# Banded attention before a routed feed-forward: q and k as two float32r pieces on two row tiles of TensorE

## The chip, the cores and the metric

One core of a Trainium2 chip runs the kernel. A core has five engines that work side by side and wait for each other by semaphores: TensorE (PE in the profile, with its weight loads as PEld), VectorE (DVE), ScalarE (ACT), GpSimd (POOL) and SyncE (SP), which here issues most DMA transfers. Matrix products land in a memory of their own, PSUM; everything else lives in SBUF, the memory that the engines share, or in DRAM. The metric is the time of one execution on the device, in microseconds (us).

## What is computed

The input is 16 sequences of 512 tokens and 128 features. Attention with 16 heads of 8 features, in which a token sees only tokens at most 128 away, is followed by a second stage that picks experts by keys. Only the first stage is touched by the change. Cut to what matters:

```python
x = L0_attn_x                                    # 16 x 512 x 128, f32
qkv = einsum('btc,oc->bto', layernorm(x), w_qkv) # q, k, v: 16 heads of 8
attn = einsum('bhqd,bhkd->bhqk', q, k) / sqrt(8)
attn = where(abs(key - query) > 128, -1e9, attn)
out = einsum('bhqk,bhkd->bhqd', softmax(attn), v)
x = x + einsum('btc,oc->bto', out, w_proj)
x = x + ffn(layernorm(x), ...)                   # batch norm, top-8 keys, experts: the second stage
```

## The kernel before

The attention stage works in units `n`: one sequence `b` and one group `g` of four heads, so 16 x 4 = 64 units, and in steps `u` of 128 tokens, four to a unit. Since the band is 128 wide, a block of 128 queries meets two or three blocks of 128 keys: 256 columns at the two ends of a sequence, 384 in the middle.

The scores are wanted in the precision of f32, but the products run in bf16. So `prepare` (L339) projects q and k of a whole sequence in f32 on TensorE, ScalarE copies them out (L348), and GpSimd splits each into three bf16 pieces whose sum is the f32 value (L362 to L370: copy, subtract, copy, subtract, each over 128 x 512). `write` (L353) stores the pieces in DRAM, and `lay` (L388) fetches them, for a unit, into the tiles `qst` and `kst`, so that the partitions hold every pairing of a q piece with a k piece: 3 x 3 x 8 = 72 rows, all four heads side by side along the free axis, three fetches for q and three for k. Rows 96 to 98 of `qst` are set to zero by one more transfer (L403), and the rows of `kst` beside them hold ones. There are six buffers of each tile; each is cleared once in whole by GpSimd (`clear`, L269).

Softmax runs in two passes over the scores. In the first, `greatest` (L409) multiplies a block of queries with its keys (a tile `s_ps` of PSUM, three buffers), and VectorE adds the band's mask and takes the row maximum in one operation (L424), which writes a scratch tile `masked` and, through a second short instruction that reads the accumulator, one column of `mx`. GpSimd negates the maxima and splits them in three bf16 pieces (`greatest_pieces`, L430), TensorE transposes these (four transposes, L447), ScalarE copies the result out (L449), and three small transfers put it in rows 96 to 98 of `qst` (L451). In the second pass, two units later, `exponentials` (L453) multiplies the keys with the queries (`e_ps`, three buffers), and the extra rows, met by the ones of `kst`, subtract the maximum; ScalarE takes the exponential (L466) into `pT`, and GpSimd clears what is outside the band (L474). `weigh` (L479) multiplies with v in f32, four heads on four column tiles of 32, into `o_ps`; `divide` (L497) transposes the result and divides by the sum.

One loop (L548 to L584) writes the order of all this out by hand. A step issues, on TensorE's queue, one s product of unit n + 2, two e products of unit n, one s product, the four weighings of an earlier step, then s, e, e, s again; after that come the pieces of maxima at u = 0, their rows at u = 1, the division at u = 2, and one piece of other work (projections and norms of sequences ahead, the output projection, the second norm). `lay` for unit n + 4 stands at u = 2. Work on TensorE and GpSimd keeps this order (`keep_in_program_order`), and a queue stands still behind its first waiting instruction. SP issues the writes, the fetches and the rows of maxima in one queue.

Of the kernel before, what the change touches and what calls it, by code (L numbers as in the profile page):

```python
# [10 lines left out]
F32 = mybir.dt.float32  # L11
BF16 = mybir.dt.bfloat16
I32 = mybir.dt.int32
# [7 lines left out]
P = 128  # L21
# [22 lines left out]
def kernel(  # L44
# [108 lines left out]
    with ExitStack() as at:  # L153
# [27 lines left out]
        for c, w in enumerate((wqT, wkT, wvT, wprojT)):  # L181
            wt = wt_ps[:, c * P : (c + 1) * P]
            if c < 2:

                w, wt = w.rearrange("p (d h) -> p d h", d=DK), wt.rearrange("p (h d) -> p d h", d=DK)
            nc.vector.tensor_copy(w, wt)
# [72 lines left out]
        NR = 96  # L259
        zeros = fix.tile([P, T], BF16, name="zeros")  # L260
        nc.gpsimd.memset(zeros, 0.0)
# [4 lines left out]
        qst = [fix.tile([P, 4, T], BF16, name=f"qst_{i}") for i in range(NBUF)]  # L266
        kst = [fix.tile([P, 4, T], BF16, name=f"kst_{i}") for i in range(NBUF)]

        def clear(i):  # L269

            nc.gpsimd.memset(qst[i].bitcast(F32), 0.0)
            nc.gpsimd.memset(kst[i].bitcast(I32), 0x3F803F80)
# [66 lines left out]
        def prepare(b):  # L339
# [13 lines left out]
            def write(what):  # L353

                via = dr.tile([3, P, T], BF16, tag=f"{what}v", name=f"{what}v_{b}")
                nc.sync.dma_start(via.rearrange("s c t -> c s t"), pieced[what, b])
                pieced[what, b] = via

            for what, full in fulls:
                pc = w2.tile([P, 3, T], BF16, tag="pc", name=f"{what}p_{b}")  # L360
                rest = w2.tile([P, T], F32, tag="rest", name=f"rest_{what}_{b}")
                pool("tensor_copy", pc[:, 0], full)  # L362
                yield
                pool("tensor_tensor", rest, full, pc[:, 0], ALU.subtract)
                yield
                pool("tensor_copy", pc[:, 1], rest)
# [3 lines left out]
                pool("tensor_tensor", pc[:, 2], rest, pc[:, 1], ALU.subtract)  # L370
# [17 lines left out]
        def lay(n):  # L388
# [4 lines left out]
            for what, st in (("q", qst[n % NBUF]), ("k", kst[n % NBUF])):  # L393
                src = pieced[what, b].rearrange("s (d h) t -> s d h t", d=DK)
                for i in range(3):
                    side = src[i if what == "q" else slice(0, 3)]
                    if what == "q":
                        side = bc(side, 0, 3)
                    nc.sync.dma_start(
                        st[3 * i * DK : 3 * i * DK + 3 * DK], side[:, :, 4 * g : 4 * g + 4]  # L400
                    )

            nc.sync.dma_start(qst[n % NBUF][NR : NR + 3], bc(zeros[0:3], 1, 4))  # L403
# [5 lines left out]
        def greatest(n, t):  # L409

            q, k = qst[n % NBUF], kst[n % NBUF]
            if t == 0:
                tops[n] = w2.tile([P, NQ, 4], F32, tag="mx", name=f"mx_{n}")
# [3 lines left out]
            for h in range(4):  # L417
                s_ps = ps_s.tile([P, 3, P], F32, tag="s", name=f"s_ps_{n}_{t}_{h}")
                s = s_ps.rearrange("p u k -> p (u k)")[:, 0:w]
                mm(  # L420
                    s, lhsT=q[:, h, t * P : (t + 1) * P], rhs=k[:, h, k0 : k0 + w],
                    start=True, stop=True,
                )
                nc.vector.tensor_tensor_reduce(  # L424
                    masked[:, 0:w], s, band.rearrange("p u k -> p (u k)")[:, from_u : from_u + w],
                    1.0, LOWEST, ALU.add, ALU.max, tops[n][:, t, h : h + 1],
                )
                yield

        def greatest_pieces(n):  # L430

            top = tops.pop(n)
            mp = w2.tile([P, NQ, 3, 4], BF16, tag="mp", name=f"mp_{n}")
            rest = w2.tile([P, NQ, 4], F32, tag="mr", name=f"mr_{n}")
            pool("tensor_scalar_mul", rest, top, -1.0)
            pool("tensor_copy", mp[:, :, 0], rest)
            pool("tensor_tensor", rest, rest, mp[:, :, 0], ALU.subtract)
            pool("tensor_copy", mp[:, :, 1], rest)
            pool("tensor_tensor", mp[:, :, 2], rest, mp[:, :, 1], ALU.subtract)
            tops[n] = mp  # L440

        def greatest_rows(n):

            mp = tops.pop(n)
            mT_ps = ps_m.tile([12, NQ, P], BF16, tag="m", name=f"mT_ps_{n}")
            for t in range(NQ):
                tr(mT_ps[:, t], mp[:, t].rearrange("p s h -> p (s h)"), ident_bf)  # L447
            mT = w2.tile([12, T], BF16, tag="mT", name=f"mT_{n}")
            nc.scalar.copy(mT, mT_ps.rearrange("r t q -> r (t q)"))  # L449
            for i in range(3):  # L450
                nc.sync.dma_start(qst[n % NBUF][NR + i : NR + i + 1], mT[4 * i : 4 * i + 4])  # L451

        def exponentials(n, u):  # L453


            q, k = qst[n % NBUF], kst[n % NBUF]
            ts = near(u)
            q0, w = ts[0] * P, len(ts) * P
            pT = w3.tile([P, 4, 3 * P], F32, tag="pT", name=f"pT_{n}_{u}")
            for h in range(4):  # L460
                e_ps = ps_e.tile([P, T], F32, tag="e", name=f"e_ps_{n}_{u}_{h}")
                mm(
# [609 lines left out]
```

## Time and profile before

| | |
|---|---|
| median of 3 runs | 1540.49 us (1539.85 to 1541.01) |
| span of the profiled execution | 1534.9 us |
| busy: PE / DVE / ACT / POOL | 1418.6 / 1347.5 / 1212.3 / 1094.3 us |
| first score product on PE | at 38.08 us |
| last masked maximum on DVE | ends at 714.3 us |
| masked maximum L424, all 1024 | 497.4 us busy, 486 ns each in the mean |
| exponential L466, all 1024 | 390.6 us busy, 436 ns each |
| s products, 1024 / e products, 1024 | 312.9 / 225.0 us busy, 307 / 301 ns each |
| rows fetched into qst, kst | 192 transfers each, 96 KB each |

The span is that of one execution that the profiler took, from its first to its last instruction; the runs are timed from outside. Busy time is the union of an engine's instructions. The records of matrix products overlap, since products are pipelined: a product's record lasts longer than the time until the next one may start, so throughput is read from start to start, not from the mean duration. An f32 product shows as two records, a bf16 one as one. A group of the profile gives line, engine, operation, tiles (out<-in), shapes and count, then busy time and mean, then the idle time of the engine before it and who ended it.

### The profile page before, as it was taken

What the parts mean: (1) busy time and instruction counts of PE and PEld (TensorE: products, weight loads), DVE (VectorE), ACT (ScalarE), POOL (GpSimd) and SP (SyncE); (2) the same over time, 40 slices, a digit from 0 to 9 for tenths busy, and PEclk for the clock granted to TensorE, in tenths of its full rate; (3) what the DMA queues carried; (4) which work ended last, traced back from release to release, by engine and by line L of the source; (5) the groups of instructions that cost most, each with busy time, mean ns of one, the idle gap of its engine ahead of it and who ended that gap; (6) DMA issues with size and microseconds to landing.
All of it is one profiled execution on the core that took longest, in us unless ns stands there. A gap on an engine that the chain in (4) does not pass through costs nothing.

```text
span 1534.9 us, 49438 instructions
## 1 busy us (share of the span) xinstructions
PE 1418.6 (92%) x16880; PEld 839.3 (55%) x16880; DVE 1347.5 (88%) x7999; ACT 1212.3 (79%) x2596; POOL 1094.3 (71%) x1706
## 2 busy tenths in 40 slices
PE   3899999999999999988689999999999999999998
PEld 1344454444444444443356666666666666666666
DVE  6778888878888888886599999999999999999994
ACT  1477777777777777778499999999999999999973
POOL 8366766667766667655287788878787888878875
PEclk9999999999999999999799999999999999999999
DMA  6243332222232222321000000000000000000000
GB/s 179 73 106 100 92 92 79 79 74 78 82 96 87 86 84 73 99 65 51 28 8 4 13 13 16 16 10 16 10 17 16 10 16 9 17 16 10 9 3 23
DMA packets 53580, 75.00 MB, mean 49 GB/s; under 512 B 5840, under 2 KB 39888, under 8 KB 53200
## 3 DMA queue, kind: packets, MB, share of 16 engines
q1 hardware_dynamic: 52496, 71.59, 16.1%
q8 instruction: 133, 2.18, 0.6%
q14 instruction: 119, 0.97, 0.2%
q10 hardware_dynamic: 832, 0.26, 0.1%
HBM read 49.28 MB, written 20.97 MB: 46 GB/s over the span
## 4 chain that ended last, share of the span: by engine, by line
DVE 48%; PE 2%; issue 1%; ACT 1%; POOL 0%; ACTq 0%
DVE idx L624 11%; DVE row L624 9%; DVE place L624 6%; DVE top L624 6%; DVE mine L624 5%; DVE best L624 4%; DVE x_ps L624 3%; DVE num L624 2%; DVE upper L624 1%; DVE zs L624 1%; PE up_ps L624 1%; PE dn_ps L624 0%; PE w_ps L624 0%; ACT L624 0%; POOL word L624 0%
## 5 line engine op out<-in xcount | busy, mean ns | idle before, releaser
L424 DVE CUSTOM_DVE_ANT_0 masked<-s_ps,band 128x384 bf16<-128x384 f32 (+1 forms) x1024 | 497.4, 486 | 126.0 <-PE s_ps L168 18.7
L466 ACT ACTIVATE pT<-e_ps 128x384 f32<-128x384 f32 (+1 forms) x1024 | 390.6, 436 | 152.8 <-PE e_ps L168 148.7
L172 POOL TENSOR_SCALAR_AFFINE_SELECT pT<-pT 128x512 f32<-128x512 f32 x384 | 238.3, 637 | 219.7 <-ACT pT L466 219.2
L168 PE MATMUL s_ps<-kst,qst 128*128 128x384 bf16 (+1 forms) x1024 | 312.9, 307 | 37.6 <-DVE mx L424 21.6
L624 POOL TENSOR_TENSOR cols<-mine,wT 64x512 f32<-64x512 bf16 x256 | 269.7, 1053 | 26.3 <-ACT row L624 6.9
L624 PE MATMUL w_ps<-cols,row 128*64 128x32 f32 x8192 | 257.3, 223 | 12.8 <-POOL cols L624 12.6
L624 PEld LDWEIGHTS w_ps<-cols,row 128*64 128x64 f32 x8192 | 249.4, 138 | 31.5 <-POOL cols L624 26.7
L624 POOL TENSOR_TENSOR g<-g,gel 128x512 f32<-128x512 f32 x128 | 163.6, 1278 | 102.2 <-ACT g L624 102.2
L168 PE MATMUL e_ps<-qst,kst 128*128 128x384 bf16 (+1 forms) x1024 | 225.0, 301 | 6.2 <-ACT pT L466 4.2
L168 PEld LDWEIGHTS <-qst 128*128 128x128 bf16 x1024 | 100.4, 98 | 197.1 <-issue 169.2
L168 PE MATMUL o_ps<-pT,vaug 128*32 128x384 f32 (+1 forms) x2048 | 191.6, 446 | 0.4 <-POOL pT L172 0.4
L624 DVE FIND_INDEX8 idx<-top,sim 128x8 uint32<-128x32 f32 x1024 | 166.2, 185 | 0.0
L624 ACT ACTIVATE row<-off_p,one 128x512 f32<-128x512 bf16 x256 | 165.9, 749 | 0.0
L624 ACT ACT_TABLE_LOAD x122 | 156.5, 1283 | 2.1
L624 DVE TENSOR_TENSOR row<-x_ps,nums_p 128x1024 f32<-128x1024 f32 x128 | 150.1, 1214 | 0.0
L624 ACT ACTIVATE off_p<-off_ps 128x512 bf16<-128x512 f32 x256 | 132.7, 602 | 18.1 <-PE off_ps L624 18.0
L624 PE MATMUL up_ps<-g,key_out_sb 64*128 64x256 f32 (+2 forms) x1152 | 146.2, 380 | 0.0
L624 PE MATMUL dn_ps<-xt,key_inT 128*64 128x256 f32 x1024 | 126.0, 389 | 2.2 <-ACT sim L624 1.3
L168 PEld LDWEIGHTS <-kst 128*128 128x128 bf16 x1024 | 98.9, 98 | 46.7 <-issue 21.1
L624 PE MATMUL off_ps<-p_bf,ident_bf 128*128 128x512 bf16 x256 | 97.5, 381 | 19.7 <-ACT p_bf L624 19.6
L624 PEld LDWEIGHTS dn_ps<-xt,key_inT 128*64 128x64 f32 x1024 | 68.5, 138 | 79.1 <-ACT row L624 43.2
L624 DVE MAX8 top<-sim 128x8 f32<-128x32 f32 x1024 | 106.6, 176 | 2.9 <-ACT sim L624 2.9
(145 smaller groups left out, 2365.0 us busy)
## 6 DMA issues: line engine op xcount, KB each, us to landing
qst<-qv SPq DMA_DIRECT2D x192, 96.0 KB
kst<-kv SPq DMA_DIRECT2D x192, 96.0 KB
qv<-qp SPq DMA_DIRECT2D x16, 384.0 KB
kv<-kp SPq DMA_DIRECT2D x16, 384.0 KB
x<-in_L_attn_x_dram SPq DMA_DIRECT2D x16, 256.0 KB
xT<-xiT SPq DMA_DIRECT2D x16, 256.0 KB
xt<-xT SPq DMA_DIRECT2D x16, 256.0 KB
out_dram<-o_sb SPq DMA_DIRECT2D x16, 256.0 KB
```

The source lines that it names most:

```text
L168: tc.keep_in_program_order(nc.tensor.matmul(*args, **kw))
L172: tc.keep_in_program_order(getattr(nc.gpsimd, op)(*args, **kw))
L424: nc.vector.tensor_tensor_reduce(masked[:, 0:w], s, band.rearrange("p u k -> p (u k)")[:, from_u : from_u + w], 1.0, LOWEST, ALU.add, ALU. ...
L466: nc.scalar.activation(pT[:, h, 0:w], e_ps[:, 0:w], AF.Exp)
L624: return lambda *args, **kw: tc.keep_in_program_order(op(*args, **kw))
```

## The change

q and k are split in two pieces of float32r (4 bytes) in place of three of bf16: copy and subtract on GpSimd, two operations in place of four. The pairings take 2 x 2 x 8 = 32 rows. Two heads lie above each other: one in rows 0 to 31, one from row 64 on, and two such pairs side by side along the free axis, so that a product of one head uses one of two row tiles of 64 of TensorE's array. One row of zeros against minus ones (row 32 or 96) makes a product 33 rows; two more rows, for the pieces of the maxima, make it 35 in the second pass. The order of products in a step is s, e, e, s as before, and takes the row tiles 0, 1, 0, 1 in turn. k is written to DRAM twice, so that one fetch per row tile brings both copies. The maxima are no longer negated, go in two pieces, and are transposed by one product of 128 columns with an identity in float32r; two transfers in place of three place them. The transfer of zeros is gone; `clear` sets one or three rows at a time, four memsets in place of two for a buffer. The weights of q and k are reordered so that heads come out in the new order.

```diff
 BF16 = mybir.dt.bfloat16
+F32R = mybir.dt.float32r
 I32 = mybir.dt.int32
...
             if c < 2:
-                w, wt = w.rearrange("p (d h) -> p d h", d=DK), wt.rearrange("p (h d) -> p d h", d=DK)
+                w = w.rearrange("p (g j d r) -> p g j d r", g=NG, j=2, r=2)
+                wt = wt.rearrange("p (g r j d) -> p g j d r", g=NG, j=2, r=2)
             nc.vector.tensor_copy(w, wt)
...
-        NR = 96
-        zeros = fix.tile([P, T], BF16, name="zeros")
-        nc.gpsimd.memset(zeros, 0.0)
+        NR, NPC = 32, 2
+        ident_r = fix.tile([P, P], F32R, name="ident_r")
+        nc.vector.tensor_copy(ident_r, ident)
         masked = fix.tile([P, 3 * P], BF16, name="masked")
         NU, NBUF = B * NG, 6
-        qst = [fix.tile([P, 4, T], BF16, name=f"qst_{i}") for i in range(NBUF)]
-        kst = [fix.tile([P, 4, T], BF16, name=f"kst_{i}") for i in range(NBUF)]
+        qst = [fix.tile([P, 2, T], F32R, name=f"qst_{i}") for i in range(NBUF)]
+        kst = [fix.tile([P, 2, T], F32R, name=f"kst_{i}") for i in range(NBUF)]
+        mps = [fix.tile([P, P], F32R, name=f"mp_{i}") for i in range(2)]
+        for mp in mps:
+            nc.gpsimd.memset(mp.bitcast(F32), 0.0)
         def clear(i):
-            nc.gpsimd.memset(qst[i].bitcast(F32), 0.0)
-            nc.gpsimd.memset(kst[i].bitcast(I32), 0x3F803F80)
+            for j in (NR, NR + P // 2):
+                nc.gpsimd.memset(qst[i][j : j + 1].bitcast(F32), 0.0)
+                nc.gpsimd.memset(kst[i][j : j + 1 + NPC].bitcast(F32), -1.0)
         clear(0)
...
             def write(what):
-                via = dr.tile([3, P, T], BF16, tag=f"{what}v", name=f"{what}v_{b}")
-                nc.sync.dma_start(via.rearrange("s c t -> c s t"), pieced[what, b])
+                times = 1 if what == "q" else 2
+                via = dr.tile([NG * 2, NPC, times, 2 * DK, T], F32, tag=f"{what}v", name=f"{what}v_{b}")
+                pc = pieced[what, b].bitcast(F32)
+                for i in range(NPC):
+                    for c in range(times):
+                        nc.sync.dma_start(via[:, i, c], pc[:, i])
                 pieced[what, b] = via
             for what, full in fulls:
-                pc = w2.tile([P, 3, T], BF16, tag="pc", name=f"{what}p_{b}")
-                rest = w2.tile([P, T], F32, tag="rest", name=f"rest_{what}_{b}")
+                pc = w2.tile([P, NPC, T], F32R, tag="pc", name=f"{what}p_{b}")
+                yield
                 pool("tensor_copy", pc[:, 0], full)
                 yield
-                pool("tensor_tensor", rest, full, pc[:, 0], ALU.subtract)
-                yield
-                pool("tensor_copy", pc[:, 1], rest)
                 if what == "k":
...
                 yield
-                pool("tensor_tensor", pc[:, 2], rest, pc[:, 1], ALU.subtract)
+                pool("tensor_tensor", pc[:, 1], full, pc[:, 0], ALU.subtract)
                 pieced[what, b] = pc
...
             for what, st in (("q", qst[n % NBUF]), ("k", kst[n % NBUF])):
-                src = pieced[what, b].rearrange("s (d h) t -> s d h t", d=DK)
-                for i in range(3):
-                    side = src[i if what == "q" else slice(0, 3)]
+                for j in range(2):
+                    side = pieced[what, b][2 * g + j].rearrange("i c (d r) t -> (i c d) (r t)", r=2)
                     if what == "q":
-                        side = bc(side, 0, 3)
-                    nc.sync.dma_start(
-                        st[3 * i * DK : 3 * i * DK + 3 * DK], side[:, :, 4 * g : 4 * g + 4]
-                    )
-            nc.sync.dma_start(qst[n % NBUF][NR : NR + 3], bc(zeros[0:3], 1, 4))
+                        side = bc(side, 0, 2)
+                    nc.sync.dma_start(st[P // 2 * j : P // 2 * j + NR].bitcast(F32), side)
         def near(t):
             return [u for u in (t - 1, t, t + 1) if 0 <= u < NQ]
-        def greatest(n, t):
-            q, k = qst[n % NBUF], kst[n % NBUF]
-            if t == 0:
-                tops[n] = w2.tile([P, NQ, 4], F32, tag="mx", name=f"mx_{n}")
+        def tile_of(j, rows):
+            return slice(P // 2 * j, P // 2 * j + rows)
+        def greatest(n, t, r, j):
+            q, k, rows = qst[n % NBUF], kst[n % NBUF], tile_of(j, NR + 1)
+            if t == r == j == 0:
+                tops[n] = w2.tile([P, 2, 2, NQ], F32, tag="mx", name=f"mx_{n}")
             us = near(t)
...
             from_u = P if t == 0 else 0
-            for h in range(4):
-                s_ps = ps_s.tile([P, 3, P], F32, tag="s", name=f"s_ps_{n}_{t}_{h}")
-                s = s_ps.rearrange("p u k -> p (u k)")[:, 0:w]
-                mm(
-                    s, lhsT=q[:, h, t * P : (t + 1) * P], rhs=k[:, h, k0 : k0 + w],
-                    start=True, stop=True,
+            s_ps = ps_s.tile([P, 3, P], F32, tag="s", name=f"s_ps_{n}_{t}_{r}_{j}")
+            s = s_ps.rearrange("p u k -> p (u k)")[:, 0:w]
+            mm(
+                s, lhsT=q[rows, r, t * P : (t + 1) * P], rhs=k[rows, r, k0 : k0 + w],
+                start=True, stop=True,
+            )
+            nc.vector.tensor_tensor_reduce(
+                masked[:, 0:w], s, band.rearrange("p u k -> p (u k)")[:, from_u : from_u + w],
+                1.0, LOWEST, ALU.add, ALU.max, tops[n][:, j, r, t : t + 1],
+            )
+        def greatest_pieces(n):
+            top, mp = tops.pop(n), mps[n % 2]
+            mp_v = mp[:, 0 : 4 * NPC * NQ].rearrange("p (j i r t) -> p j i r t", j=2, i=NPC, r=2)
+            pool("tensor_copy", mp_v[:, :, 0], top)
+            pool("tensor_tensor", mp_v[:, :, 1], top, mp_v[:, :, 0], ALU.subtract)
+            tops[n] = mp
+        def greatest_rows(n):
+            mp = tops.pop(n)
+            half = 2 * NPC * NQ
+            mT_ps = ps_m.tile([P, P], F32, tag="m", name=f"mT_ps_{n}")
+            mm(mT_ps, lhsT=mp, rhs=ident_r, start=True, stop=True)
+            mT = w2.tile([2 * half, P], F32R, tag="mT", name=f"mT_{n}")
+            nc.scalar.copy(mT, mT_ps[0 : 2 * half])
+            for j in range(2):
+                at_j = P // 2 * j + NR + 1
+                nc.sync.dma_start(
+                    qst[n % NBUF][at_j : at_j + NPC].bitcast(F32), mT[half * j : half * j + half].bitcast(F32)
                 )
-                nc.vector.tensor_tensor_reduce(
-                    masked[:, 0:w], s, band.rearrange("p u k -> p (u k)")[:, from_u : from_u + w],
-                    1.0, LOWEST, ALU.add, ALU.max, tops[n][:, t, h : h + 1],
-                )
-                yield
-        def greatest_pieces(n):
-            top = tops.pop(n)
-            mp = w2.tile([P, NQ, 3, 4], BF16, tag="mp", name=f"mp_{n}")
-            rest = w2.tile([P, NQ, 4], F32, tag="mr", name=f"mr_{n}")
-            pool("tensor_scalar_mul", rest, top, -1.0)
-            pool("tensor_copy", mp[:, :, 0], rest)
-            pool("tensor_tensor", rest, rest, mp[:, :, 0], ALU.subtract)
-            pool("tensor_copy", mp[:, :, 1], rest)
-            pool("tensor_tensor", mp[:, :, 2], rest, mp[:, :, 1], ALU.subtract)
-            tops[n] = mp
-        def greatest_rows(n):
-            mp = tops.pop(n)
-            mT_ps = ps_m.tile([12, NQ, P], BF16, tag="m", name=f"mT_ps_{n}")
-            for t in range(NQ):
-                tr(mT_ps[:, t], mp[:, t].rearrange("p s h -> p (s h)"), ident_bf)
-            mT = w2.tile([12, T], BF16, tag="mT", name=f"mT_{n}")
-            nc.scalar.copy(mT, mT_ps.rearrange("r t q -> r (t q)"))
-            for i in range(3):
-                nc.sync.dma_start(qst[n % NBUF][NR + i : NR + i + 1], mT[4 * i : 4 * i + 4])
-        def exponentials(n, u):
-            q, k = qst[n % NBUF], kst[n % NBUF]
+        def exponentials(n, u, r, j):
+            q, k, rows = qst[n % NBUF], kst[n % NBUF], tile_of(j, NR + 1 + NPC)
             ts = near(u)
             q0, w = ts[0] * P, len(ts) * P
-            pT = w3.tile([P, 4, 3 * P], F32, tag="pT", name=f"pT_{n}_{u}")
-            for h in range(4):
-                e_ps = ps_e.tile([P, T], F32, tag="e", name=f"e_ps_{n}_{u}_{h}")
-                mm(
-                    e_ps[:, 0:w], lhsT=k[:, h, u * P : (u + 1) * P], rhs=q[:, h, q0 : q0 + w],
-                    start=True, stop=True,
-                )
-                nc.scalar.activation(pT[:, h, 0:w], e_ps[:, 0:w], AF.Exp)
-                if h % 2:
-                    yield
+            if (n, u) not in probs:
+                probs[n, u] = w3.tile([P, 4, 3 * P], F32, tag="pT", name=f"pT_{n}_{u}")
+            e_ps = ps_e.tile([P, T], F32, tag="e", name=f"e_ps_{n}_{u}_{r}_{j}")
+            mm(
+                e_ps[:, 0:w], lhsT=k[rows, r, u * P : (u + 1) * P], rhs=q[rows, r, q0 : q0 + w],
+                start=True, stop=True,
+            )
+            nc.scalar.activation(probs[n, u][:, 2 * r + j, 0:w], e_ps[:, 0:w], AF.Exp)
+        def outside_band(n, u):
+            ts = near(u)
             for t in ts:
                 if t != u:
-                    side = pT[:, :, (t - ts[0]) * P : (t - ts[0] + 1) * P]
+                    side = probs[n, u][:, :, (t - ts[0]) * P : (t - ts[0] + 1) * P]
                     sign = 1 if t < u else -1
...
                     )
-            probs[n, u] = pT
         def weigh(n, u):
...
                 load(1)
-            tops_of = greatest(n + AHEAD, u) if 0 <= n + AHEAD < NU else iter(())
-            probs_of = exponentials(n, u) if 0 <= n < NU else iter(())
-            next(tops_of, None)
-            next(probs_of, None)
-            next(tops_of, None)
-            if 0 <= s - LATE < NU * NQ:
-                weigh(*divmod(s - LATE, NQ))
-            together(tops_of, probs_of)
+            for r in range(2):
+                for what, j in ((greatest, 0), (exponentials, 1), (exponentials, 0), (greatest, 1)):
+                    of = n + AHEAD if what is greatest else n
+                    if 0 <= of < NU:
+                        what(of, u, r, j)
+                if r == 0 and 0 <= s - LATE < NU * NQ:
+                    weigh(*divmod(s - LATE, NQ))
+            if 0 <= n < NU:
+                outside_band(n, u)
             free = True
```

## The prediction

> **What bounds the kernel now.** The table by stage comes first; its columns are the stretch, busy us (instructions) of PE, PEld, DVE, ACT and POOL, the granted clock, the DMA share and GB/s.
>
> ```profile
> 0.00:38.50 38.50, 14.33 (x31) 6.24 (x32) 23.12 (x154) 6.43 (x12) 31.18 (x47) 1.00 0.69 179
> 38.50:714.30 675.80, 639.42 (x4985) 311.70 (x4983) 559.55 (x2370) 483.38 (x1219) 433.87 (x852) 1.00 0.29 84
> 714.30:748.50 34.20, 24.86 (x173) 11.81 (x170) 11.25 (x36) 18.71 (x45) 14.07 (x25) 0.80 0.11 39
> 748.50:1534.90 786.40, 740.02 (x11698) 509.55 (x11696) 753.52 (x5442) 703.82 (x1320) 615.16 (x784) 0.99 0.05 13
> ```
>
> Only the first three rows are touched. In the second, 64 units of four heads take 675.8 / 64 = 10.56 us each. PE is 95% busy there and DVE 83%, which points at PE. The timeline of DVE says otherwise:
>
> ```profile
> 406.55 0.56 DVE L424 CUSTOM_DVE_ANT_0 masked<-s_ps,band 128x384 bf16<-128x384 f32 x1
> 407.03 0.08 DVE L424 DVE_READ_ACCUMULATOR2_ANT mx<- 128x1 f32 x1
> 407.26 0.56 DVE L424 CUSTOM_DVE_ANT_0 masked<-s_ps,band 128x384 bf16<-128x384 f32 x1
> ...
> 407.96 0.56 DVE L424 CUSTOM_DVE_ANT_0 masked<-s_ps,band 128x384 bf16<-128x384 f32 x1
> ```
>
> A 384-wide masked maximum starts every 0.71 us and a 256-wide one every 0.576, whatever PE does: the operation, the read of its accumulator, and 0.14 us in which DVE waits for itself. Eight of each make 8 x 0.709 + 8 x 0.576 = 10.28 us a unit; the 0.28 left to 10.56 is divisions and norms that do not fit into those 0.14 us. So DVE sets the pace. In the groups of that stretch (busy, mean ns | idle before, releasers) PE left it waiting for 18.7 us, of which 9.8 are the start:
>
> ```profile
> L424 DVE CUSTOM_DVE_ANT_0 masked<-s_ps,band 128x384 bf16<-128x384 f32 (+1 forms) x1024 | 497.4, 486 | 126.0 <-PE s_ps L168 18.7 <-DVE mx L424 6.4 <-PE e_ps L168 0.5
> L168 PE MATMUL s_ps<-kst,qst 128*128 128x256 bf16 x1023 | 312.8, 307 | 26.7 <-DVE mx L424 21.6 <-DMA kst<-kv 0.6 <-DMA qv<-qp 0.3
> L168 PE MATMUL o_ps<-pT,vaug 128*32 128x256 f32 (+1 forms) x1968 | 184.1, 446 | 0.0
> ```
>
> Taking off 0.144 per entry for its own wait, real starvation is about 7 us, most of it where ACT reloads its tables (1.28 us twice) and PE stands behind an e product.
>
> **What PE needs.** From start to start in the trace of one unit: an s or e product takes 0.162 (384) or 0.109 (256), so 16 x (0.162 + 0.109) = 4.34. Four sets of weighings (L488, four column tiles side by side) take 2 x 0.654 + 2 x 0.440 = 2.19, plus 0.096 at each change of array shape, eight of them: 2.96. The transposes of L505 take 4 x 0.109 = 0.44, the maxima's (L447) 0.41 with their changes, a batch's norms and projections 4.82 / 4 = 1.20. Sum 9.35 of 10.56: PE is 1.2 us a unit below DVE.
>
> **The change, part by part.** DVE's instructions are not touched: the 1024 maxima keep size, order and waits; one copy of an identity is added at the start. So the 10.28 stands, and a lighter PE can return only the 7 us.
>
> PE, score products. No row has float32r. Bounds: bf16 at one cycle a column (0.162 for 384) and f32 q_ps at 0.86 for 512, four. The f32 transposes, single records of 4-byte data, take two (0.109 for 128). For the overlap of two row tiles of 64 the second stage has the row:
>
> ```profile
> 1002.82 1.14 PE L624 MATMUL up_ps<-g,key_out_sb 64*128 64x256 f32 x8
> 1002.82 0.73 PEld L624 LDWEIGHTS up_ps<-g,key_out_sb 64*128 64x128 f32 x8
> ```
>
> Eight records of 0.209 fit into four, in pairs that start 0.007 apart; only the first pair after a change of shape takes 0.313, by 0.104 of weight loading that nothing covers. The rows read as halves: an f32 product costs two by two, an f32 transpose two by one; a piece already rounded to float32r should have one half, so I take one by one, like bf16, and full overlap: a unit's eight bursts of four products cost 8 x 0.104 + 4 x 2 x 0.162 + 4 x 2 x 0.109 = 3.00 in place of 4.34. Added: changes of shape around work that shared the full array: 0.19 for L505, 7 x 0.19 / 4 = 0.34 for the batch. The maxima's transposes fall from 0.41 to 0.35. PE then needs 2.96 + 0.44 + 1.20 + 3.00 + 0.53 + 0.35 = 8.5. Ends: without overlap, or at two cycles with it, 4.34 + 0.83 for 3.00 makes 10.65; four cycles overlapped 15.0; four alone 23.7. Below 8.5 nothing is gained, since DVE stays at 10.28.
>
> A rule speaks against this. The Trainium skill (TensorE: Matmul & The Clock Gate, "Part 3: Packing small matmuls — row/col tiling", what overlaps) lets a weight load overlap only products on other rows; the trace has up_ps load 0.002 after its own tile's product started. By the rule each burst pays 0.104 twice and PE needs 9.3, by the row 8.5; both are below DVE.
>
> POOL and SP, at the start. The chain to the first maximum:
>
> ```profile
> 26.84 1.16 POOL L172 TENSOR_TENSOR kp<-rest_k,kp 128x512 bf16<-128x512 f32 x1
> ...
> 28.04 0.36 SPq L356 DMA_DIRECT2D kv<-kp  x1
> ...
> 38.08 1.27 PE L168 MATMUL s_ps<-kst,qst 128*128 128x256 bf16 x4 [10.91 <-DMA kst<-kv]
> ...
> 38.49 0.42 DVE L424 CUSTOM_DVE_ANT_0 masked<-s_ps,band 128x256 bf16<-128x256 f32 x1 [9.80 <-PE s_ps L168]
> ```
>
> Before, eight operations for pieces (0.61 or 1.16) and seven long memsets or norms end at 28.0. After, in the built order: q copy 14.95, memset 15.5, subtract 17.3, k copy 18.4, two memsets, subtract 20.9 to 22.1: 5.9 earlier. Two memsets a buffer become four of one or three rows, as long a row and so taken at 0.9 each: the first two buffers end at 10, before q is there; the other sixteen stand behind these pieces. Against it, k goes out in four writes for one: two of 256 KB follow the last subtract for 384 KB, 128 KB at the 180 GB/s of the start = 0.7, and one issue of 0.39; the rows are fetched by four issues in place of six (-0.8) with three for zeros gone. Net -5.8; ends 0 (the doubled k is late by as much) and -7.6 (the second batch's pieces).
>
> Later, POOL loses 3.5 us a batch and 0.7 a unit, ACT's copy of the maxima shrinks, SP issues 4 + 2 for 7 + 3 a unit: all beside DVE, 0. If that cover went, the queue behind SP's wait for the maxima holds the next unit's fetches, used one and a half units (15 us) later.
>
> End stretch (714 to 748): products in pairs free about 1 us. Starvation: of 7 us the table loads stay; 1.5 returned.
>
> The clock: PE's lower load has a price. One window of this stretch ran at half clock:
>
> ```profile
> 335.12:338.53 3.41, 1.85 (x14) 0.47 (x12) 2.88 (x15) 3.37 (x6) 1.52 (x3) 1.00 0.43 145
> 338.53:341.94 3.41, 3.31 (x18) 1.42 (x18) 1.73 (x8) 1.34 (x5) 1.76 (x2) 0.50 0.46 131
> ```
>
> The first was filled by streaming columns for 0.355 of its time (columns times passes at 2.4 a ns), then came 3.41 us at half. Other windows at 0.391 kept the clock; half-clock ones returned at 0.86, not at 0.735. With products in pairs the median falls from 0.78 to 0.58, with 3 to 5 of 179 windows below 0.39, at the table loads. Each costs about 1 us of starvation: +3 for three more.
>
> The skill's same page ("Part 1: The HAM clock gate") has the clock fall after an idle window; here it fell after a 36% one. By the page the +3 would be 0.
>
> Sum: -5.8 - 1.5 - 1 + 3 = -5.3. The profiled span 1534.9 becomes 1529.6; the runs' median is 5.6 above it (1540.49), so **1535 us**.
>
> **Rivals.** (1) Two cycles a column, or one without overlap: PE at 10.65 passes DVE. For: 4-byte transposes. Against: up_ps pairs. Of the 1.2 us a unit that PE now stands behind DVE and ACT I leave a third, 0.45: 11.1 a unit, +0.54 x 64 = +35, less 6: 1570. It decides once PE is over 10.3.
> (2) The half clock stays. At half clock PE needs 2 x 6.0 of streaming, some 15 changes of shape at 0.137 (0.347 from product to weighing at 339.2, of which 0.213 streams) and eight loads of 0.15: 15.3 a unit. That streams 0.78, between the 0.735 that stayed half and the 0.86 that returned, so a cold spell may last. If a quarter of the 198 windows are cold, each loses 3.41 x (15.3 - 10.28) / 15.3 = 1.1 us: +54, less 6: 1588. For it: the share now falls by 0.2. Against it: the median stays at 0.58. It decides where many windows fall below 0.39.
> (3) Four cycles, overlapped: (15.0 - 10.56) x 64 = +284: 1820. For: the operands stay 4 bytes wide, as in q_ps. Against: the halves above.
> (4) The start's 5.8 is eaten by the k writes and the cold windows: 1540, unchanged. For: the fetches at 38 wait on DMA, not on POOL alone. Against: only 128 KB more follows the last subtract.
>
> **How the numbers follow.** Forecast 57%, (1) 18%, (2) 10%, (3) 5%, (4) 10%. About 0.2% (3 us) is what runs of this kernel can tell from nothing. Faster 0.53 (the forecast less its upper end), same 0.12, slower 0.35. The forecast's own range is 1526 to 1541; to leave out 2 in 10 the range reaches 1580, into (1) and (2).
>
> **What would show it.** Right: starts of maxima still 0.576 and 0.71 apart, first one near 32.7, last near 710; s and e pairs 0.007 apart, 0.16 a pair; PE waiting for DVE more. Wrong: DVE idle for s_ps by tens of us; pairs 0.32 or more apart; half clock over more than ten windows.

## The result and the profile after

| | before | after |
|---|---|---|
| median of the runs side by side | 1540.17 us | 1755.9 us (1735.77 to 1779.32, 4 runs) |
| ratio, 95% interval | | 1.1314 [1.1272, 1.1355] |
| span of the profiled execution | 1534.9 us | 1777.6 us |
| first masked maximum starts | 38.49 us | 38.19 us |
| last masked maximum ends | 714.3 us | 942.9 us |

The change made the kernel 13% slower, against a forecast of 1535. The ratio takes only the two faster runs of the changed kernel (the other two are over 1.5% above its fastest), while the profiled execution is the slowest of the four. The executions of the changed kernel scatter by 2.5%, those of the kernel before by 0.1%, and roughly with the mean granted clock: 0.794 at 1779.3 us, 0.819 at 1764.7, 0.817 at 1747.1, 0.825 at 1735.8.

The table by stage of the changed kernel (columns as in the prediction: stretch, busy us of PE, PEld, DVE, ACT and POOL, granted clock, DMA share, GB/s):

```profile
0.00:38.20 38.20, 14.95 (x31) 6.34 (x31) 23.21 (x155) 6.33 (x12) 30.82 (x46) 1.00 0.78 212
38.20:942.90 904.70, 897.95 (x4793) 438.41 (x4792) 567.93 (x2370) 477.37 (x1219) 351.39 (x613) 0.63 0.23 70
942.90:985.00 42.10, 35.53 (x162) 16.11 (x162) 9.65 (x31) 19.20 (x44) 14.93 (x23) 0.50 0.07 26
985.00:1777.60 792.60, 748.33 (x11710) 515.36 (x11706) 755.19 (x5448) 703.97 (x1321) 613.51 (x782) 0.98 0.05 13
```

Nearly the whole loss is in the second row: 904.7 us for 675.8, +229 (the shortest run was 44 us below this one as a whole). DVE does the same work there (567.9 for 559.6 us), PE is busy for 99% of it, and the clock column has gone from 1.00 to 0.63. The start is the same length, the end stretch 8 us longer, all of it at half clock, the second stage 6 us longer. The page's slices say the same; each digit is the granted clock of a fortieth of the span:

```profile
PEclk9858555677755559566555899999999999999989
```

The clock is recorded in steps of 3.41 us, called windows here. Summed from these records, 666 us of the attention stage ran at half clock; in the kernel before it was one window. The records miss one stretch: before a run's first record (at 62.0 us in the kernel before, at 75.8 in the changed one) the column prints 1.00, but the products run at half speed. Two f32 products of q take twice as long there, as the kernel before shows:

```profile
22.29 2.07 PE L168 MATMUL q_ps<-xnT,wqT 128*128 128x512 f32 x2 [0.67 <-ACT xnT L336]
...
65.28 1.02 PE L168 MATMUL q_ps<-xnT,wqT 128*128 128x512 f32 x2
```

So some 24 us of half clock come on top before the change and 38 after it: 27 against 703 us in all.

What the same burst of products (the four score products that a step issues in a row) costs at the two clocks is on PE's timeline. Two bursts at half clock, then two at full (the row with x2 holds the two e products):

```profile
500.59 0.69 PE L169 MATMUL s_ps<-kst,qst 33*128 33x384 f32 x1
500.60 1.00 PE L169 MATMUL e_ps<-qst,kst 35*128 35x384 f32 x2
501.08 0.52 PE L169 MATMUL s_ps<-kst,qst 33*128 33x384 f32 x1
501.53 0.47 PE L169 MATMUL mT_ps<-ident_r,mp 128*128 128x128 f32 x1
...
676.94 0.39 PE L169 MATMUL s_ps<-kst,qst 33*128 33x256 f32 x1
676.94 0.50 PE L169 MATMUL e_ps<-qst,kst 35*128 35x256 f32 x2
677.16 0.28 PE L169 MATMUL s_ps<-kst,qst 33*128 33x256 f32 x1
```

At half clock the first pair of 384 columns takes 0.49 us (0.164 of load that nothing covers, and 0.320 = 384 columns at 1.2 a ns), the second 0.45 up to the next work. At full clock the first pair of 256 takes 0.22 (0.110 and 0.107). The two products of a pair start at most 0.004 apart. So float32r takes one cycle a column, as bf16 did before (0.162 us for 384), the row tiles overlap, and the load is paid once a burst: the price list of the prediction holds at both clocks. On VectorE the same stretch looks like this:

```profile
500.08 0.56 DVE L428 CUSTOM_DVE_ANT_0 masked<-s_ps,band 128x384 bf16<-128x384 f32 x1
...
501.32 0.56 DVE L428 CUSTOM_DVE_ANT_0 masked<-s_ps,band 128x384 bf16<-128x384 f32 x1 [0.67 <-PE e_ps L169]
...
502.03 0.56 DVE L428 CUSTOM_DVE_ANT_0 masked<-s_ps,band 128x384 bf16<-128x384 f32 x1
...
502.74 0.56 DVE L428 CUSTOM_DVE_ANT_0 masked<-s_ps,band 128x384 bf16<-128x384 f32 x1
```

Where VectorE is served, its maxima still start 0.71 apart; where PE is late they wait for it. Over the whole run (busy, mean ns | idle before, first releaser):

```profile
L428 DVE CUSTOM_DVE_ANT_0 masked<-s_ps,band 128x384 bf16<-128x384 f32 (+1 forms) x1024 | 497.6, 486 | 293.1 <-PE e_ps L169 160.1
```

PE has taken DVE's place as the bound. From one unit's division to the next, units at full clock take 10.3 to 10.7 us, those wholly at half clock mostly 14 to 17.

Which windows lose the clock? These two rows of the changed kernel follow each other:

```profile
328.43:331.84 3.41, 3.40 (x30) 1.72 (x29) 3.32 (x15) 2.86 (x8) 0.66 (x2) 1.00 0.12 50
331.84:335.25 3.41, 3.41 (x24) 2.02 (x20) 2.81 (x15) 1.22 (x4) 2.33 (x4) 0.50 0.32 61
```

PE is busy through all of the first and streams columns for 0.61 of it (columns times passes at 2.4 a ns, a pair counted once), and yet 3.41 us at half follow. In the kernel before, a window of the second stage (at 795.9 us) kept the clock at 0.39, and the lowest of the attention stage at 0.45. A sum over all recorded windows of the changed kernel's stage: 16 full-clock windows lost it, at shares of 0.29 to 0.60; the 43 that kept it lie at 0.56 and more. And it comes back seldom: of 195 windows at half clock, 180 were followed by another, at shares up to 0.83.

### The profile page after: what moved, and what is told of

It is laid out like the page before. It is cut to its first block, busy times and chain, and to the rows that moved or that the text cites. A ratio compares the mean times of both kernels' runs of the same rounds, so it can differ in the third digit from the quotient of the medians.

```text
span 1777.6 us, 48737 instructions
## 1 busy us (share of the span) xinstructions
PE 1696.8 (95%) x16688; PEld 976.2 (55%) x16688; DVE 1356.0 (76%) x8000; ACT 1206.9 (68%) x2596; POOL 1010.6 (57%) x1463
## 5 line engine op out<-in xcount | busy, mean ns | idle before, releaser
L169 PE MATMUL s_ps<-kst,qst 33*128 33x384 f32 (+1 forms) x1024 | 432.0, 501 | 12.5 <-DMA kst<-kv 9.4
L169 PEld LDWEIGHTS s_ps<-kst,qst 33*128 33x128 f32 x1024 | 232.0, 268 | 332.3 <-DVE mx L428 217.2
L169 PE MATMUL e_ps<-qst,kst 35*128 35x384 f32 (+1 forms) x1024 | 405.4, 494 | 4.3 <-ACT pT L468 1.9
L169 PE MATMUL o_ps<-pT,vaug 128*32 128x384 f32 (+1 forms) x2048 | 292.9, 660 | 0.0
L169 PEld LDWEIGHTS e_ps<-qst,kst 35*128 35x128 f32 x1024 | 221.8, 269 | 25.3 <-ACT pT L468 21.8
```

What stands on the lines that cost most here:

```text
L169: tc.keep_in_program_order(nc.tensor.matmul(*args, **kw))
```

## The experiments

The theory after this result: the clock is granted by how many rows of the array work, and for how long. A float32r product uses 33 or 35 rows, a pair 66 to 70 of 128, where the bf16 product before used all. Rivals: float32r itself, two row tiles at once, and too little work on PE, whatever rows it uses. Diffs are against the changed kernel, unless another is named. "Half clock" is the sum over the attention stage from the clock's records; the stretch ahead of the first record adds 24 to 40 us in each run (5 in the kernel before with three scratch tiles), at the spacing of half clock throughout.

**One row tile at a time.** The four products of a burst go to one row tile, so that none overlap.

```diff
-            for r in range(2):
-                for what, j in ((greatest, 0), (exponentials, 1), (exponentials, 0), (greatest, 1)):
+            for j in range(2):
+                for what, r in ((greatest, 0), (exponentials, 0), (exponentials, 1), (greatest, 1)):
```

> The changed kernel with the order of products turned so that the four between two weighings lie on one row tile: the same products, but none beside another. If the overlap is what makes PE too idle (T1): clock back above 0.95, 1530 to 1580. If a product on 64 rows counts little, overlapped or not (T2), or a float32r product does (T3): clock stays low, and the lost overlap at half clock adds some 2 us a unit, above 1800.

Measured: 2119.9 us, ratio 1.3786 [1.3676, 1.3896]; the last maximum ends at 1282.6. PE's timeline:

```profile
503.39 0.69 PE L169 MATMUL s_ps<-kst,qst 33*128 33x384 f32 x1
503.88 0.84 PE L169 MATMUL e_ps<-qst,kst 35*128 35x384 f32 x2
504.52 0.52 PE L169 MATMUL s_ps<-kst,qst 33*128 33x384 f32 x1
504.96 0.47 PE L169 MATMUL mT_ps<-ident_r,mp 128*128 128x128 f32 x1
```

After the first product (0.49 with its load) they follow 0.32 apart, two in 0.64: 384 columns at 1.2 a ns, half clock, and that spacing goes through the stage. (The page prints a clock of 1.00 here: the first clock record of this run is at 1329.6 us, after the stage. The spacing decides.) Overlap is not what costs the clock: without it PE streams for more of the time, with half as many rows at once, and the clock is worse.

**Float32r over the whole array.** Products run over 97 and 101 rows, no row tiles, and so sum the scores of the two heads of a pair.

```diff
         def tile_of(j, rows):
-            return slice(P // 2 * j, P // 2 * j + rows)
+            return slice(0, P // 2 + NR + 1 + 2 * (rows - NR - 1))
```

(`clear` sets whole tiles, and the maxima lie in rows 97 to 100.)

> The changed kernel with score products over 97 or 101 rows of the whole array in float32r, one after the other, no row tiles (a product sums the two heads that lie above each other and subtracts both maxima, so its output is another). If few rows are what makes a product count little for the clock (T2): clock above 0.95 in the attention stage, 1530 to 1580. If float32r does it (T3): clock low, above 1900, as in series on one row tile (2120).

Measured: 1564.19 us, ratio 1.0166 [1.0139, 1.0194]; half clock 11 us, last maximum at 734.9. Against the run before, in which the products also follow one by one, type and columns are the same and only the rows are more: the clock is back. Float32r is not the cause.

**Half the rows in bf16.** In the kernel before, both products take rows 0 to 63 only, which leaves out part of the pairings and the subtraction of the maxima.

```diff
-                    s, lhsT=q[:, h, t * P : (t + 1) * P], rhs=k[:, h, k0 : k0 + w],
+                    s, lhsT=q[0:64, h, t * P : (t + 1) * P], rhs=k[0:64, h, k0 : k0 + w],
```

(and the same for the e products)

> The kernel before, with its bf16 score products cut to rows 0 to 63 (the pairings and maxima in the other rows are left out), one after the other as before, nothing else changed. T2 (a product on 64 rows counts little): clock falls in the attention stage, time above 1650. T1 and T3: 1535 to 1555, clock as before.

Measured: 1601.64 us (two runs, 1585.95 and 1617.33, so 3 to 5% slower), less than the 1650 expected. The profiled run, of 1617.33 us, has 120 us at half clock, nearly all in three long spells; the mean granted clock is 0.943 in it and 0.972 in the other, against 0.983 to 0.996 in the runs of the kernel before beside them. No type and no order was changed. Fewer rows alone lose the clock, and time.

**Work added to keep the clock.** Before each step's first s product, three bf16 products over the full array into the same tile, which the s product then overwrites; and a second kernel with one.

```diff
+            if r == j == 0:
+                for _ in range(FILL):
+                    mm(s, lhsT=ident_bf, rhs=band.rearrange("p u k -> p (u k)")[:, 0:w], start=True, stop=True)
```

> The changed kernel with three more bf16 products over the whole array (128 rows, the width of the step) in front of each step's first score product, overwritten by it: some 107 us of pure extra PE streaming at full clock. Theory 'clock' (PE's counted activity is too low, so it is given half the clock for most of the stage): mean clock of the attention stage back above 0.95, time falls to 1535 to 1570 although work is added. Rival 'load' (float32r products and changes of array shape are simply more than PE can do, the clock is a side show): time rises, above 1800.

> The changed kernel with one bf16 product over the whole array in front of each step's first score product, in place of three. Clock theory: between the two points known (none: 1756, three: 1643), or below both if three had already made PE the bound at full clock; half-clock time in the attention stage between 85 and 666 us. Load theory: above 1756.

Measured: with three, 1642.88 us, ratio 1.0684 [1.0612, 1.0756], 85 us at half clock; with one, 1656.0, ratio 1.0763 [1.0669, 1.0857], 222 us. Against a ratio of 1.1314 for the changed kernel, PE does more work in less time, which no bound by load would allow. With three, more than the 1535 to 1570 expected was left; what else the added products cost was not taken apart. That rows count, and not any work on PE, these two runs alone do not tell.

**All rows of each row tile.** The first pass takes 62 rows of its row tile and the second 64; the added rows hold zeros of q against minus ones of k, the maxima move to the last two, and `clear` sets whole tiles. The result is the same.

```diff
-            q, k, rows = qst[n % NBUF], kst[n % NBUF], tile_of(j, NR + 1)
+            q, k, rows = qst[n % NBUF], kst[n % NBUF], tile_of(j, P // 2 - NPC)
...
-                at_j = P // 2 * j + NR + 1
+                at_j = P // 2 * j + P // 2 - NPC
...
-            q, k, rows = qst[n % NBUF], kst[n % NBUF], tile_of(j, NR + 1 + NPC)
+            q, k, rows = qst[n % NBUF], kst[n % NBUF], tile_of(j, P // 2)
```

> The changed kernel with each product taken over all rows of its row tile (62 in the first pass, 64 in the second; the rows added hold zeros against minus ones, the maxima lie in the last two), all else alike. Theory A, the clock goes by how many rows a product uses: a pair now uses 126 to 128 rows for 66 to 70, so the clock stays near full (0.95 or more), the last maximum ends near 715 to 735 and the time is 1530 to 1560. Theory B, a product on a row tile counts as little whatever rows it uses, or zeros do not count: half clock over 500 us or more, the last maximum near 900, 1700 to 1780. Between these, 1600 to 1680 with 100 to 300 us at half clock, the rows count, but zeros against minus ones count for less than data.

Measured: 1576.04 us, ratio 1.027 [1.0227, 1.0314], above the 1530 to 1560 expected; half clock 44 us, last maximum at 743.1. The table by stage:

```profile
35.30:743.10 707.80, 685.75 (x4794) 354.09 (x4794) 562.62 (x2370) 462.14 (x1219) 345.05 (x606) 0.97 0.30 91
743.10:790.00 46.90, 37.94 (x190) 17.28 (x189) 14.62 (x74) 23.01 (x50) 16.00 (x24) 0.64 0.08 29
```

Rows that add nothing but zeros take the ratio from 1.1314 to 1.027, four fifths of the loss. The windows that lost the clock now streamed for 0.32 to 0.47 of their time, those that kept it for 0.45 and more.

The traces of the thirteen runs with clock records in the stage (all here but the one on one row tile at a time) show how the rows count. Weigh every stretch in which columns stream by the rows in use over 128, a pair of row tiles by the rows of both, and add up by window. Of 2107 full-clock windows, those that lost the clock then lie at 0.40 or less and those that kept it at 0.37 or more, whatever the kernel; a bound of 0.38 puts 11 on the wrong side. Without the weight the losers reach 0.60 while others kept it from 0.39, and the best bound misplaces 45. This is a sum over modelled starts, so the proportion to the rows holds within its few hundredths only.

**The same with zeros on both sides.** From the kernel with all rows: the added rows of k are zero too.

```diff
             nc.gpsimd.memset(kst[i].bitcast(F32), -1.0)
+            for j in (NR, NR + P // 2):
+                nc.gpsimd.memset(kst[i][j : j + P // 2 - NR - NPC].bitcast(F32), 0.0)
```

> The kernel with all rows of each row tile, with the 29 or 30 added rows of k set to zero in place of minus one, so that zeros meet zeros in them. Theory A1 (the clock counts the rows that a product takes, whatever they hold): as with minus ones, 40 to 90 us at half clock in the attention stage, 1570 to 1590. Theory A2 (it counts what the rows hold, since the zeros against minus ones still moved data): most of the half clock of the changed kernel returns, 400 us or more, 1680 to 1760. Between these, the contents count in part.

Measured: 1570.02 us, ratio 1.0187 [1.0153, 1.0222]; half clock 34 us. Whether the added rows of k hold zeros or minus ones does not matter, only that the product takes them.

What is left in the kernel with all rows: against the kernel before, the stage is 32 us longer and its end 13 us longer (clock 0.64 there). VectorE's waits for PE beyond its own 0.144 make some 31 us after the start, about half of them at half clock and half at full clock. The second kind is many short ones; the two looked at closely, of 0.24 and 0.51 us, stand behind an f32 projection that holds PE's queue for 1.05 us before the burst.

**k written once.** From the kernel with all rows: k goes to DRAM once, and four fetches that repeat 16 source rows replace two.

```diff
-                times = 1 if what == "q" else 2
+                times = 1
...
+                        for i in range(NPC):
+                            nc.sync.dma_start(
+                                st[P // 2 * j + NR // 2 * i : P // 2 * j + NR // 2 * i + NR // 2].bitcast(F32),
+                                bc(side[2 * DK * i // 2 : 2 * DK * i // 2 + DK], 0, 2),
+                            )
```

> The kernel with all rows of each row tile, with k written to DRAM once (two writes in place of four) and fetched in four transfers in place of two. If the doubled writes of k ate what the shorter split gained at the start: the first maximum starts 3 to 6 us earlier than the 38.2 of the changed kernel, near 33 to 35, and the time is 2 to 6 us below that of the same kernel with k written twice. If the fetches themselves or the queue's issues set the start: first maximum within 1 us of 38, the same time.

A miss on both sides: 1670.25 us, ratio 1.0851 [1.0805, 1.0897], 94 us slower than with k written twice. The fetch of k is issued 3.9 us earlier (26.0 for 29.9), but the first maximum starts at 36.4, no earlier than with k written twice (35.3, and 36.3 in the run with three scratch tiles, whose start is the same). A stretch of 20 us, in the columns of the table by stage, shows why:

```profile
374.00:394.00 20.00, 16.89 (x96) 7.35 (x94) 10.38 (x45) 10.44 (x27) 5.10 (x11) 0.83 0.13 52
```

And in the list of waits (who waited for whom: us in total, times, longest):

```profile
PE e_ps L169 <- DMA qst<-mT: 51.2, 22, 5.1
```

Where only fetches that repeat their rows run, 0.13 of the DMA engines are busy, as much as two of 16, and some 50 GB/s are moved. Of the 600 us from 60 on, 362 ran so (slices of 2 us with 0.10 to 0.15 busy at 40 to 60 GB/s), against 140 with k written twice. The two small transfers of the maxima come late behind these fetches, e products wait 51 us for them, and half clock rises from 44 to 188 us: stalls make windows with a low share.

The Trainium skill has the rule for it (DMA: Bandwidth & Descriptors, "Rules for kernel authors"): a transfer is spread over engines by its outermost dimension, so a leading broadcast of c copies stays on at most c engines. Here c is 2, and the 0.13 agrees.

**Three scratch tiles.** The prediction has VectorE wait 0.14 us for itself between maxima. Here the scratch tile `masked` is one of three in turn, in the kernel before, in the changed one, and in the one with all rows.

```diff
-        masked = fix.tile([P, 3 * P], BF16, name="masked")
+        maskeds = [fix.tile([P, 3 * P], BF16, name=f"masked_{i}") for i in range(3)]
```

> The kernel before with three scratch tiles in turn for the masked scores in place of one: the next maximum no longer waits for VectorE's own last write. If DVE sets the pace as predicted (0.576 and 0.709 from start to start, of which 0.144 a wait for itself): starts 0.43 to 0.5 and 0.57 to 0.62 apart, PE at 9.35 us a unit becomes the limit, attention 64 x 9.6 to 10, total 1480 to 1510. If PE sets it: 1535 to 1545.

> The changed kernel with the same three scratch tiles. A faster DVE asks more of PE, so PE is counted busier: if the clock is lost for lack of counted activity, part of it comes back: 1480 to 1680, with less time at half clock than 666 us. If the clock is lost for another reason, PE at half clock stays the limit: 1740 to 1770.

> The kernel with all rows of each row tile, and three scratch tiles for the masked maximum in turn. Theory A (the clock follows the rows): VectorE starts its maxima 0.35 and 0.49 us apart, PE needs 8.5 us a unit and the other work of VectorE fits into the gaps, so a unit takes 9.3 to 9.8 us: last maximum near 630 to 665, 1470 to 1500, below the 1504 of the kernel before with three scratch tiles. Theory B (the clock stays low): as the changed kernel with three scratch tiles, 1660 to 1720.

Measured: 1503.84 us for the kernel before, ratio 0.9783 [0.9757, 0.981], last maximum at 673.8; 1695.1 (1666.33 to 1714.47) for the changed one, still with 381 us at half clock in the profiled run, of 1666.33 us; 1550.82 for all rows, ratio 1.0062 [1.0029, 1.0095]. VectorE's timeline in the first:

```profile
404.48 0.55 DVE L424 CUSTOM_DVE_ANT_0 masked<-s_ps,band 128x384 bf16<-128x384 f32 x1
404.96 0.08 DVE L424 DVE_READ_ACCUMULATOR2_ANT mx<- 128x1 f32 x1
404.96 0.55 DVE L424 CUSTOM_DVE_ANT_0 masked<-s_ps,band 128x384 bf16<-128x384 f32 x1
```

Maxima start 0.48 apart for 0.71: the 0.14, and the read of the accumulator, which now overlaps the next operation, are gone. So VectorE did set the pace before, as predicted. The third kernel missed its 1470 to 1500: 109 us at half clock, and waits that the list puts to the transfers of the maxima:

```profile
PE e_ps L169 <- DMA qst<-mT: 29.8, 17, 3.6
```

**q written twice as well.** From that kernel: no fetch repeats its rows any more.

```diff
-                        nc.sync.dma_start(via[:, i, c], pc[:, i])
+                        nc.sync.dma_start(via[:, c, i] if what == "q" else via[:, i, c], pc[:, i])
...
-                    if what == "q":
-                        side = bc(side, 0, 2)
```

> The kernel with all rows of each row tile and three scratch tiles, with q too written to DRAM twice, so that no fetch repeats its source rows. In the run with k written once, fetches that repeat 16 source rows ran for long stretches at 50 GB/s with the DMA engines 0.13 busy, and e products waited for the maxima's rows behind them; with three scratch tiles they still waited 30 us so, and 109 us of the attention stage were at half clock. Theory F (the repeated fetch of q holds up the maxima's rows, and these waits cost clock): the wait for those rows falls below 8 us, the stretches at 50 GB/s go, half clock falls to 40 to 80 us, the last maximum ends 25 to 50 us earlier than 724, and the time is 1505 to 1530. Rival (the rows come late for another reason, such as the short lead of the second pass over a faster first one): the wait stays at 20 us or more and the time at 1540 to 1565.

Measured: 1501.94 us (1491.65 to 1503.08), ratio 0.9758 [0.9732, 0.9784], better than expected. The wait for the maxima's rows is 3.7 us, once; 4 of the 600 us run near 50 GB/s by the count above (146 with q written once); half clock 41 us; last maximum at 669.3:

```profile
35.00:669.32 634.32, 614.38 (x4797) 314.09 (x4796) 520.08 (x2361) 457.85 (x1217) 345.30 (x607) 0.97 0.39 114
```

So the change, with all rows, three scratch tiles and q written twice, beats the kernel before by 2.4%. But the scratch tiles alone do as much for the kernel before (0.9783, intervals overlap): the float32r pieces themselves have not been shown to save time. Nor did the kernel before get the same help: its fetch of q repeats its rows three times (`bc(side, 0, 3)` in the diff of the change), and no run takes that out.

## Why the prediction was wrong

- *DVE sets the pace at 10.28.* Right for the kernel before (three scratch tiles take 40 us off its stage) and for the changed kernel's units at full clock (10.3 to 10.7 us).
- *PE at 8.5: one cycle a column, full overlap, 0.104 per burst.* The terms were right, as the bursts above show. On the weight load, the rule that was weighed (a load overlaps only products on other rows) lost to the row: with one row tile at a time, products on the same rows follow 0.32 apart, which is their streaming alone. What did not follow is "below 8.5 nothing is gained" read as "nothing is lost": with all rows, VectorE still waits some 15 us for PE at full clock, where the sum had starvation fall by 1.5. PE serves in order, and a mean need below DVE's does not keep a long projection from standing before a burst.
- *Start -5.8.* Measured -0.3. The pieces of k were ready 4.8 us earlier (23.2 for 28.0), but SP's fetch of k went out at 31.5:

```profile
20.33 4.12 SPq L366 DMA_DIRECT2D kv<-kp  x4
26.43 1.34 SPq L405 DMA_DIRECT2D qst<-qv  x2
31.54 0.82 SPq L405 DMA_DIRECT2D kst<-kv  x2
```

  The term "128 KB more" was too small: q's and k's writes are 1.5 MB, which move at 200 GB/s from 20 to 30 us, with the DMA engines about half busy. Rival (4) named the place, but k written once showed that the writes are only half of it; a fetch that repeats its rows is as late. `clear` seems to have a part too: with two whole-tile memsets for a buffer the first maximum came at 35.2 to 36.9 in five runs, with the four short ones at 37.6 to 38.8 in five, and with two whole and two of 30 rows at 38.1. Which transfer or memset sets it was not taken apart further.
- *The clock, +3.* This is the step that failed: "3 to 5 of 179 windows below 0.39". In place of +3 the stage took 229 us more, and the end stretch, put at -1, took 8 more at half clock. The share was foreseen well (a median of 0.58; the full-clock windows have 0.62), but it counted a pair on 66 to 70 rows like a product on 128. The bound of 0.39 came from a window of the second stage with products on all 128 rows, and was carried to products with half the rows. 195 of the 254 recorded windows were at half clock, not three more.
- *Rival (2), "the half clock stays".* The right outcome with the right price: 15.3 us a unit at half clock against 14 to 17 measured, and 195 windows at its 1.1 us make 215 of the 229. Its count, a quarter of the windows, and its 10% were too low. Its condition, many windows below 0.39, did not come as it was put: 15 of the 16 windows that lost the clock streamed for 0.50 of their time or more. They are low only when the rows are counted, which neither the forecast nor this rival did. The half-clock share of 0.78, "between the 0.735 that stayed and the 0.86 that returned", was in the prediction; with few rows, 0.83 stayed.
- *The Trainium skill* (TensorE: Matmul & The Clock Gate, "Part 1: The HAM clock gate"). By the page the clock falls after an idle window and the term is 0. Here PE was busy for 3.40 of 3.41 us in a window that lost it; the runs decide against a reading by busy time.

## What to carry to other kernels

Before a product is cut to fewer rows, ask what the clock will make of it: a row-tiled product that is cheaper by its columns can cost TensorE half its clock, and it is then slower for everything else on it. If rows are free, take them all, with zeros: a pair of 256 columns took 0.22 us at full clock on 33 and 35 rows and on 62 and 64 alike, and the ratio fell from 1.1314 to 1.027 here. Read the granted clock by stage before any other column, and when an engine off the path is made lighter, ask what its share of work was holding up.

## What the runs showed of the hardware that was not expected

- The clock follows streaming weighted by the rows in use, not busy time. Half clock in the attention stage, by the clock's records: 3.4 us with bf16 on 128 rows, 11 with float32r on 97 to 101, 34 and 44 on 124 to 128 in two row tiles (with less streaming), 120 with bf16 on 64, 666 on 66 to 70 in two row tiles, and, by the spacing of the products, all of it on 33 to 35 at a time.
- By share of time it is lost more easily than regained: with all rows, lost at a streaming share below about 0.45, regained only at 0.74 to 0.83. Counted in columns on 128 rows this is no asymmetry: over the thirteen runs the best bounds are 0.38 at full clock and 0.74 at half, and since a window of 3.41 us holds 8190 columns at full clock and half as many at half, both are some 3,000 to 3,100 columns a window. The bound at half clock is the rougher one: it misplaces 42 of 556 windows.
- Every run was at half clock until its first clock record, at 43 to 78 us (at 1330 us on one row tile at a time), although the profile prints 1.00 there.
- DMA fetches that repeat 16 source rows ran at about 50 GB/s with 0.13 of the DMA engines busy; writing q twice and fetching it plainly took 1550.8 to 1501.9 us.
- A single scratch tile that nobody reads cost VectorE 0.14 us a maximum, and the overlap with the read of its accumulator: 2.2% of the kernel.
